# The last attention of an eight-layer model in half rounds: scores of one pair of kv heads at a time, a longer pipeline, and the second softmax's maximum taken inside the addition

## The chip, the cores and the metric

The kernel is one program on one core of a Trainium2 chip. It computes four blocks, each an attention and a feed-forward part, for eight sequences of 256 tokens of width 256, all in fp32 (masks and some one-hot matrices are bf16). The metric is the device time of one execution in microseconds. Engines are named as the profile names them: PE (TensorE matmul), PEld (its weight loads), DVE (VectorE), ACT (ScalarE), POOL (GpSimd) and SP (SyncE, which issues most DMAs).

## The reference

Only the last attention (L3) matters here. It is a differential attention: 16 query heads and 4 kv heads, each head with two parts of 16 columns. Each part has its own causal softmax; the second, weighted by a learned factor for each head, is subtracted from the first, and the difference, causal again, goes through one more softmax before it multiplies V.

```python
x = _layernorm(x + _L2_ffn_ref(x, ...), axis=-1)
x = _layernorm(x + _L3_attn_ref(x, Wq, Wk, Wv, Wo, lq1, lq2, lk1, lk2, rms_w), axis=-1)
x = _layernorm(x + _L3_ffn_ref(x, gate, gate_up_proj, down_proj), axis=-1)

def _L3_attn_ref(x, ...):              # 16 heads, 4 kv heads, D = 16
    q = _rope((x @ Wq).reshape(b, s, H, 2 * D))
    k = _rope((x @ Wk).reshape(b, s, KVH, 2 * D))
    v = (x @ Wv).reshape(b, s, KVH, D)
    ...                                # k and v repeated 4 times, heads cut in two parts
    energy = jnp.einsum('bqhad,bkhad->bahqk', qd, kd)
    energy = jnp.where(causal, NEG, energy)
    scores = jax.nn.softmax(energy / np.sqrt(D), axis=-1)
    diff = scores[:, 0] - lam * scores[:, 1]
    diff = jnp.where(causal, NEG, diff)
    diff = jax.nn.softmax(diff, axis=-1)
    att = jnp.einsum('bhqv,bvhd->bqhd', diff, v)
    att = att * jax.lax.rsqrt(jnp.mean(att * att, -1, keepdims=True) + EPS) * rms_w
    att = att * (1.0 - LAM_INIT)
    return att.reshape(b, s, E) @ Wo
```

## The kernel before

The eight layers run one after the other. The layers changed here are written in a manual schedule: on each engine the instructions stand in the order in which the Python code issues them, and the framework adds the waits. So the order of calls in the loop of `attn3` is the order of each engine's queue.

**Units.** `attn3` works on 48 units, six for each of the eight sequences (a batch, below). A unit is one block of 128 queries (`qc` 0 or 1) and some of the four heads that share a kv head: two heads with 128 keys when `qc` is 0 (two units), one head with 256 keys when `qc` is 1 (four units). All four kv heads, `s` in the code, are in each unit. The projections put kv head `s` in the 32 partitions from 32 s on, so the four score matmuls of a round use four 32-row strips of the PE array, and each writes its own PSUM bank.

**PSUM.** One pool has four tags of two banks each: `t` (projections, transposes), `a` and `s` (scores), `o` (two banks that `attn3` holds throughout: `bank_o` for the values, `bank_x` for V and the ends).

**What a unit does, by method of `Unit`:**
- `scores`: L651 matmuls for all four kv heads (two records each in the profile, since fp32 takes two passes), L664 a bf16 matmul that adds the causal mask, L668 a DVE reduction of each bank to the maximum, L671 the exponentials on ACT with their sums (each followed by an accumulator read).
- `factors`: L681 the reciprocals of the sums on DVE; on POOL L686, which masks the diagonal block, and L691 and L692, which make the factor `c` from the sums and the head's weight.
- `differences`, in two halves of two kv heads: L705 on DVE adds `c` times the second part's exponentials to the first's; L709 on DVE reduces the result to its maximum; L710 on POOL scales the maximum; L713 on POOL writes `v`, the scaled difference less its maximum.
- `turned`: L730 transposes `v` on PE, L732 takes the exponential on ACT straight from PSUM into `p`.
- `values`: L746 multiplies by V into `bank_o`, on 32-column strips; the ones beside V give the sum. L751 copies the result out when a query block is complete.

**The ends of a batch.** `finish(b)` is a generator whose steps the loop spreads over later units. It turns the result back (L764), divides (L768, L769), squares (L776), then does the RMS norm (L781 to L798), transposes (L805), multiplies by Wo (L814), adds the residual and normalizes. After the fourth batch it appends the sort of the next layer's tokens (`ffn3_sort`) to the queue `others`; that is router matmuls (L1959), top-4, ranks (`place`, L903 to L959) and then 32 row scatters issued by POOL (L986), three a unit.

**The loop.** In step n: `factors` of unit n-1, one step of `others`, `scores` of unit n, `values` of unit n-3, a projection step of the next batch (`project`: L607 matmuls, L611 DVE multiplication by the rotary tables, L625 V), `differences` of unit n-1 with another projection step and one step of `ends` between its halves, two steps of `others` unless rows are being scattered, `turned` of unit n-2. When the loop ends, what is left of `ends` and `others` is handed to `ffn3`, whose first fetch of rows (SP, L2012) waits for the scatter and for the last values.

## Time and profile before

| what | value |
|---|---|
| time, median of 3 runs | 2415.38 us (2408.47 to 2417.45) |
| the profiled execution | 2415.87 us, of it 2414.2 us span |
| busy in the span | PE 90%, DVE 59%, ACT 43%, POOL 38% |
| last attention, first L651 to last L746 | 1671.7 to 2102.8 us |
| an even batch in it (1813.4 to 1861.2 us) | 47.8 us; DVE 43.7, PE 42.5, ACT 34.8, POOL 33.2 busy |
| the batch with the sort beside it (1912.4 to 1978.6 us) | 66.2 us; DVE 57.2, PE 50.0 busy |
| granted PE clock in these two | 0.93 and 0.79 |

Busy shares over the whole span mix eight layers with different limits, so they say little of this one; a stretch of one batch is the right size, because all its work repeats every six units. PE's busy time counts a matmul from its start to a modelled end, so matmuls that overlap are counted once and short gaps vanish in it. For what PE's work really needs, one looks at how long after one group the next one starts when nothing is waited for. In the groups of instructions the columns are: line, engine, operation, output and input, shape, count; then busy us and mean ns of one; then the engine's idle time just before it, with what ended that. In the order of time they are start, duration, engine, line, operation.

### The profile page before, as it was taken

The page shows a single profiled execution, that of the slowest core. Times are in us where ns is not written, and L with a number is a line of the kernel's source. Part 1 is how long each engine was busy: PE and PEld are TensorE (multiplying, and loading weights), DVE is VectorE, ACT ScalarE, POOL GpSimd, SP SyncE. Part 2 cuts the span into 40 slices and gives each one's busy share as a digit, 9 for nine tenths or more (in the row PEclk, how much of TensorE's full clock was granted, in tenths as well). Part 3 has the DMA queues.
Part 4 walks back from the last instruction along what each step waited for, and adds up shares of the span by engine and source line. Part 5 has one row for each costly group of instructions (what it writes and reads, how often), then busy time and mean ns, then how long its engine had stood idle before and what let it go on. Part 6 is the DMA issues. An engine that isn't in the chain of part 4 may idle for free.

```text
span 2414.2 us, 36482 instructions
## 1 busy us (share of the span) xinstructions
PE 2166.5 (90%) x11920; PEld 1479.6 (61%) x11920; DVE 1432.6 (59%) x3998; ACT 1034.1 (43%) x2999; POOL 913.6 (38%) x1711
## 2 busy tenths in 40 slices
PE   7999889999999999999999999999889877689880
PEld 4555688857676676676654465556556654367760
DVE  4566486754644554544574444766998987553454
ACT  1334355554544544544441112223767746444340
POOL 1222444353433423433312311001666658616444
PEclk9999999999999999999999999999999978799995
DMA  5000411100000010000340011002000001255652
GB/s 166 1 1 1 168 41 46 46 24 3 3 3 3 3 54 1 1 1 1 131 160 1 0 53 54 1 1 107 1 2 1 2 3 43 67 149 189 214 174 81
DMA packets 92311, 120.78 MB, mean 50 GB/s; under 512 B 9757, under 2 KB 79582, under 8 KB 91102
## 3 DMA queue, kind: packets, MB, share of 16 engines
q1 hardware_dynamic: 82270, 95.75, 12.2%
q0 software_dynamic: 8192, 21.11, 2.8%
q8 instruction: 100, 1.64, 0.3%
q10 hardware_dynamic: 1664, 1.57, 0.2%
q14 instruction: 85, 0.70, 0.1%
HBM read 67.53 MB, written 50.88 MB: 49 GB/s over the span
## 4 chain that ended last, share of the span: by engine, by line
PE 26%; DVE 10%; POOL 7%; issue 3%; ACT 2%; DMA 2%; SPq 0%; POOLq 0%; another core or an unknown queue 0%; DVEq 0%; ACTq 0%
PE ps_a L2031 4%; PE ps_s L1842 2%; PE ps_a L1842 2%; POOL v L713 2%; PE ps_o L2053 2%; PE ps_a L1638 2%; PE ps_s L1638 2%; PE ps_o L1889 2%; DVE e L705 2%; ACT e L671 2%; DVE nmd L709 1%; DVE nm L668 1%; PE ps_t L2023 1%; POOL rows L986 1%; DVE bnst L200 1%
## 5 line engine op out<-in xcount | busy, mean ns | idle before, releaser
L1429 POOL TENSOR_SCALAR p<-p,rs 128x128 f32<-128x128 f32 (+1 forms) x256 | 104.9, 428 | 254.5 <-DVE rs L1427 155.8
L1419 ACT ACTIVATE p<-p,nms,rq 128x128 f32<-128x128 f32 (+1 forms) x256 | 137.7, 539 | 132.6 <-DVE nms L1415 132.3
L1343 ACT ACTIVATE sq<-ps_a 128x512 f32<-128x512 f32 x126 | 74.6, 592 | 195.5 <-PE ps_a L1335 195.2
L148 POOL TENSOR_SCALAR rsq<-bnmv 128x2 f32<-128x2 f32 x61 | 12.9, 211 | 379.3 <-DVE bnmv L201 364.1
L671 ACT ACTIVATE e<-ps_a,nm 128x128 f32<-128x128 f32 (+1 forms) x256 | 106.0, 437 | 105.6 <-DVE nm L668 95.6
L1344 DVE TENSOR_REDUCE ssk<-sq 128x4 f32<-128x512 f32 x64 | 43.8, 686 | 171.1 <-ACT sq L1343 170.9
L713 POOL TENSOR_SCALAR v<-e,r,nmd 128x128 f32<-128x128 f32 (+1 forms) x256 | 134.4, 537 | 10.0
L2031 PE MATMUL ps_a<-w_f_gup,xTg 128*128 x504 | 111.1, 344 | 17.0 <-DVE xTg L2025 5.9
L705 DVE SCALAR_TENSOR_TENSOR e<-e,c 128x128 f32<-128x128 f32 (+1 forms) x256 | 101.3, 446 | 38.9 <-POOL c L692 38.8
L1335 PE MATMUL ps_a<-w_a_wq,xT 128*128 128x512 f32 x256 | 122.5, 601 | 1.7 <-DVE k L1357 1.7
L1335 PE MATMUL ps_a<-w_a_wv,xT 128*128 128x512 f32 x256 | 120.8, 593 | 0.6 <-ACT q L1368 0.6
L1335 PE MATMUL ps_a<-w_a_wk,xT 128*128 128x512 f32 x248 | 116.5, 593 | 0.0
L1467 PE MATMUL ps_o<-w_a_wo,attT 128*128 128x256 f32 x512 | 111.8, 379 | 0.0
L730 PE MATMUL ps_t<-ident,v 128*128 128x128 f32 x384 | 68.7, 311 | 48.0 <-DVE qT L611 8.9
L671 ACT ACTIVATE e<-ps_s,nm 128x128 f32<-128x128 f32 (+1 forms) x256 | 107.1, 454 | 0.0
L1467 PEld LDWEIGHTS ps_o<-w_a_wo,attT 128*128 128x128 f32 x512 | 96.7, 190 | 12.8
L1195 DVE SCALAR_TENSOR_TENSOR yg<-ps_t,xg,yg 128x128 f32<-128x128 f32 x266 | 93.2, 350 | 17.9 <-PE ps_t L1184 8.4
L2031 PEld LDWEIGHTS ps_a<-w_f_gup,xTg 128*128 128x128 f32 x504 | 81.4, 195 | 29.6 <-issue 9.8
L1402 PE MATMUL ps_s<-kT,qT 128*128 128x256 f32 (+1 forms) x512 | 99.4, 327 | 0.0
L1344 DVE TENSOR_REDUCE ssq<-sq 128x4 f32<-128x512 f32 x64 | 43.8, 685 | 91.9 <-ACT sq L1343 91.9
L1184 PE MATMUL ps_t<-w_f_w,hg 128*128 x608 | 83.4, 281 | 10.1 <-DVE yg L1195 6.2
L730 PEld LDWEIGHTS ps_t<-ident,v 128*128 128x128 f32 x384 | 49.8, 160 | 64.5 <-POOL v L713 19.1
(418 smaller groups left out, 6008.7 us busy)
## 6 DMA issues: line engine op xcount, KB each, us to landing
rows<-zero SPq DMA_DIRECT2D x42, 384.0 KB
xg<-rows SPq DMA_DIRECT2D x42, 384.0 KB
outs<-yg SPq DMA_DIRECT2D x42, 384.0 KB
w_f_gup<-in_f_gup SPq DMA_DIRECT2D x8, 768.0 KB
w_f_w<-in_f_w SPq DMA_DIRECT2D x8, 512.0 KB
w_f_down<-in_f_down SPq DMA_DIRECT2D x8, 384.0 KB
w_f_up<-in_f_up SPq DMA_DIRECT2D x5, 512.0 KB
lrows<-zero SPq DMA_DIRECT2D x12, 204.0 KB
```

Of the source, the lines that this page charges most:

```text
L671: nc.scalar.activation(e[:, s, j * nk : (j + 1) * nk], sc[s][:, j, :], AF.Exp, bias=nm[:, s, j : j + 1], scale=1.0, accum_out=sums[:, s, j ...
L705: nc.vector.scalar_tensor_tensor(d[:, s, h, :], u.e[:, s, h, 1, :], u.c[:, s, h : h + 1], d[:, s, h, :], ALU.mult, ALU.add,)
L713: nc.gpsimd.tensor_scalar(u.v[:, s, h, :], d[:, s, h, :], u.r[:, s, h, 0:1], nm[:, s, h : h + 1], ALU.mult, ALU.add,)
L730: nc.tensor.transpose(ps[:, s, c, :], x, self.ident)
L1335: nc.tensor.matmul(ps, self.xt(u.b, t, c), w[which][:, c, u.cols], start=(c == 0), stop=(c == 1),)
L1402: nc.tensor.matmul(sc[:, j, :], u.qT[:, h0 + j, qc * P : (qc + 1) * P], u.kT[:, h0 + j, 0:nk], start=True, stop=True,)
L1419: nc.scalar.activation(u.p[qc][:, h0 + j, :], u.p[qc][:, h0 + j, :], AF.Exp, bias=nm[:, j : j + 1], scale=r[:, j : j + 1], accum_out=u.sum ...
L1429: nc.gpsimd.tensor_scalar(u.p[qc][:, j, :], u.p[qc][:, j, :], ri[:, j : j + 1], 1.0, ALU.mult, ALU.mult,)
L1467: nc.tensor.matmul(y[:, t, :], attTs[b][:, h, t * P : (t + 1) * P], w["wo"][:, h, :], start=(h == 0), stop=(h == 15),)
L1638: nc.tensor.matmul(x, xT[:, c, tok], w[name][:, c, cols], start=(c == 0), stop=(c == 1),)
L1842: nc.tensor.matmul(x, w[name][:, c, cols], xT[:, c, :], start=(c == 0), stop=(c == 1))
L2031: nc.tensor.matmul(ps, xT[j][:, c, :], w["gup"][:, bass.ds(er[j], 1), c, :].rearrange("p o f -> p (o f)"), start=(c == 0), stop=(c == 1),)
```

## The change

The score banks move into a pool of their own (`psum_as`), which is closed and opened again around `attn3`; inside it the pool holds two tiles of two banks, tag `pair`, instead of `a` and `s`. The tile of exponentials gets four buffers instead of three, and `v` is gone.

A unit is now done in two halves, each of one pair of kv heads:
- `scores(u, i)` does the matmuls of two strips into one pair of banks, both masks, one reduction over both banks and the exponentials.
- `factors` also multiplies, on POOL, the second part's exponentials by `c`, in place.
- `differences(u, i)` is one DVE operation for each head: it adds the two parts, scales by the first part's reciprocal and keeps the running maximum. POOL then casts the maxima to bf16.
- `turned(u, i)` transposes the differences and, into the same accumulation, multiplies the broadcast bf16 maximum by a negated identity (`nidentb`), which subtracts it from each column; then the exponential as before. The softmax does not depend on the value that is subtracted, so the rounded maximum serves.

In step n the loop does, for each half: `scores` of unit n, `turned` of unit n-3 (behind the matmuls, ahead of the reduction), in the second half `factors` of unit n-1, then `differences` of unit n-2 and projection, sort and end steps; `values` are those of unit n-4. The loop is one step longer. The first steps of `finish` become `gather`, called for each query block by itself, both through `bank_x`.

```diff
+    def open_pairs(self):
+        self.psum_as = self.pairs.enter_context(
+            self.tc.tile_pool(
+                name="psum_as", bufs=2, space=bass.MemoryType.PSUM, reuse_waits="tile"
+            )
+        )
+
     def ps(self, tag):
-        return self.psum.tile([P, 512], F32, tag=tag, name=f"ps_{tag}")
+        pool = self.psum_as if tag in "as" else self.psum
+        return pool.tile([P, 512], F32, tag=tag, name=f"ps_{tag}")
...
         bank_o, bank_x = self.ps("o"), self.ps("o")
+        nidentb = act.tile([P, P], BF16, tag="nidentb", name="nidentb", bufs=1)
+        nc.gpsimd.tensor_scalar(nidentb, self.identb, -1.0, None, ALU.mult)
...
-            def scores(u):
+            def scores(u, i):
 
                 qT, kT = qTs[u.b], kTs[u.b]
                 nk, nj = u.nk, 2 * u.nh
-                ps = [self.ps("as"[s % 2]) for s in range(4)]
+                if i == 0:
+                    u.nm = self.small.tile([P, 4, nj], F32, tag="nm3", name="nm3")
+                    u.sums = self.small.tile([P, 4, u.nh, 2], F32, tag="sums", name="sums")
+                    e = act.tile([P, 4, 512], F32, tag="e", name="e", bufs=4)
+                    u.e = e.rearrange("p s (h a k) -> p s h a k", h=u.nh, a=2)
+                two = slice(2 * i, 2 * i + 2)
+                ps = self.psum_as.tile([P, 2, 512], F32, tag="pair", name="ps_pair")
+                sc = ps.rearrange("p s (j k) -> p s j k", j=nj)
+                e = u.e[:, two].rearrange("p s h a k -> p s (h a) k")
+                sums = u.sums[:, two].rearrange("p s h a -> p s (h a)")
                 for j in range(nj):
-                    for s in range(4):
-                        r = slice(32 * s, 32 * s + 32)
+                    for s in range(2):
+                        r = slice(64 * i + 32 * s, 64 * i + 32 * s + 32)
                         nc.tensor.matmul(
-                            ps[s][:, j * nk : (j + 1) * nk],
+                            sc[:, s, j, :],
                             qT[r, 2 * u.h0 + j, u.qc * P : u.qc * P + P],
                             kT[r, j % 2, :nk],
                             start=(j == 0), stop=False,
                         )
-                nm = self.small.tile([P, 4, nj], F32, tag="nm3", name="nm3")
-                u.sums = self.small.tile([P, 4, u.nh, 2], F32, tag="sums", name="sums")
-                sums = u.sums.rearrange("p s h a -> p s (h a)")
-                e = act.tile([P, 4, 512], F32, tag="e", name="e", bufs=3)
-                u.e = e.rearrange("p s (h a k) -> p s h a k", h=u.nh, a=2)
-                sc = [x.rearrange("p (j k) -> p j k", j=nj) for x in ps]
-                for s in range(4):
+                for s in range(2):
                     nc.tensor.matmul(
-                        sc[s][:, :, nk - P :], self.identb, self.maskA[:, :nj, :],
+                        sc[:, s, :, nk - P :], self.identb, self.maskA[:, :nj, :],
                         start=False, stop=True,
                     )
-                    nc.vector.tensor_reduce(nm[:, s, :], sc[s], AX.X, ALU.max, negate=True)
-                for s in range(4):
+                yield
+                nm = u.nm[:, two]
+                nc.vector.tensor_reduce(nm, sc, AX.X, ALU.max, negate=True)
+                for s in range(2):
                     for j in range(nj):
                         nc.scalar.activation(
-                            e[:, s, j * nk : (j + 1) * nk], sc[s][:, j, :], AF.Exp,
+                            e[:, s, j, :], sc[:, s, j, :], AF.Exp,
                             bias=nm[:, s, j : j + 1], scale=1.0,
                             accum_out=sums[:, s, j : j + 1],
                         )
+                yield
 
             def factors(u):
 
                 g = nc.gpsimd
                 u.r = self.small.tile([P, 4, u.nh, 2], F32, tag="r3", name="r3")
                 nc.vector.reciprocal(u.r, u.sums)
-                u.c = self.small.tile([P, 4, u.nh], F32, tag="c3", name="c3")
-
+                c = self.small.tile([P, 4, u.nh], F32, tag="c3", name="c3")
+                g.tensor_tensor(c, u.sums[:, :, :, 0], u.r[:, :, :, 1], ALU.mult)
+                g.tensor_tensor(c, c, nlam[:, :, u.h0 : u.h0 + u.nh], ALU.mult)
                 for i in range(2):
                     diag = u.e[:, 2 * i : 2 * i + 2, :, 0, u.nk - P :]
                     g.affine_select(
                         diag, diag, pattern=[[0, 2], [0, u.nh], [-1, P]],
                         compare_op=ALU.is_ge, fill=NEG, base=0, channel_multiplier=1,
                     )
-                    if i == 0:
-                        g.tensor_tensor(u.c, u.sums[:, :, :, 0], u.r[:, :, :, 1], ALU.mult)
-                        g.tensor_tensor(
-                            u.c, u.c, nlam[:, :, u.h0 : u.h0 + u.nh], ALU.mult
-                        )
-
-            def differences(u):
-
-                d = u.e[:, :, :, 0, :]
-                u.v = act.tile([P, 4, u.nh, u.nk], F32, tag="v", name="v", bufs=3)
-                nm = self.small.tile([P, 4, u.nh], F32, tag="nmd", name="nmd")
-                for i in range(2):
-                    two = slice(2 * i, 2 * i + 2)
                     for s in (2 * i, 2 * i + 1):
                         for h in range(u.nh):
-                            nc.vector.scalar_tensor_tensor(
-                                d[:, s, h, :], u.e[:, s, h, 1, :], u.c[:, s, h : h + 1],
-                                d[:, s, h, :], ALU.mult, ALU.add,
-                            )
-                    nc.vector.tensor_reduce(nm[:, two], d[:, two], AX.X, ALU.max, negate=True)
-                    nc.gpsimd.tensor_tensor(nm[:, two], nm[:, two], u.r[:, two, :, 0], ALU.mult)
...
+                            x = u.e[:, s, h, 1, :]
+                            g.tensor_scalar(x, x, c[:, s, h : h + 1], 1.0, ALU.mult, ALU.mult)
+
+            def differences(u, i):
+
+                if i == 0:
+                    u.mx = self.small.tile([P, 4, u.nh], F32, tag="nmd", name="nmd")
+                    u.mb = [
+                        act.tile([P, 2, u.nh], BF16, tag="nmb", name="nmb", bufs=4)
+                        for _ in range(2)
+                    ]
+                for s in (2 * i, 2 * i + 1):
+                    for h in range(u.nh):
+                        d = u.e[:, s, h, 0, :]
+                        nc.vector.tensor_tensor_reduce(
+                            out=d, in0=d, in1=u.e[:, s, h, 1, :],
+                            scale=u.r[:, s, h, 0:1], scalar=2 * NEG,
+                            op0=ALU.add, op1=ALU.max, accum_out=u.mx[:, s, h : h + 1],
+                        )
+                nc.gpsimd.tensor_copy(u.mb[i], u.mx[:, 2 * i : 2 * i + 2])
+
+            def turned(u, i):
+
+                if i == 0:
+                    u.p = []
+                ps = self.ps("t").rearrange("p (s c q) -> p s c q", s=2, c=2)
+                for s in range(2):
+                    for c in range(2):
+                        x = (
+                            u.e[:, 2 * i + s, c, 0, :] if u.qc == 0
+                            else u.e[:, 2 * i + s, 0, 0, c * P : (c + 1) * P]
+                        )
+                        nc.tensor.matmul(
+                            ps[:, s, c, :], x, self.ident, is_transpose=True,
+                            start=(s == 0 and c == 0), stop=False,
+                        )
+                for s in range(2):
+                    for h in range(u.nh):
+                        most = u.mb[i][:, s, h : h + 1].to_broadcast([P, P])
+                        out, one = ps[:, s, h, :], nidentb
+                        if u.qc == 1:
+                            out = ps[:, s]
+                            one = nidentb.unsqueeze(1).to_broadcast([P, 2, P])
+                        nc.tensor.matmul(
+                            out, most, one, start=False, stop=(s == 1 and h == u.nh - 1)
+                        )
+                p = act.tile([P, 2, 2, P], F32, tag="p", name="p", bufs=4)
+                nc.scalar.activation(
+                    p.rearrange("p s c q -> p (s c q)"),
+                    ps.rearrange("p s c q -> p (s c q)"), AF.Exp,
+                )
+                u.p += [p[:, 0], p[:, 1]]
...
-                    if u.qc == 1:
-                        done.append(finish(u.b))
...
+        def gather(b, qc):
...
+            pt = bank_x.rearrange("p (h s d) -> p h s d", h=4, s=4)
...
         def finish(b):
...
+            if b == NB - 1:
+                gather(b, 1)
+                yield
+            att, sqs = atts[b], squares[b]
...
-        for n in range(len(units) + 3):
+        for n in range(len(units) + 4):
 
             def at(back):
                 return units[n - back] if 0 <= n - back < len(units) else None
 
-            u, last = at(0), at(1)
+            u = at(0)
             if u and u.qc == 0 and u.h0 == 0:
                 step(projections, 100)
                 if u.b + 1 < NB:
                     projections.append(project(u.b + 1))
-            if last:
-                last.factors()
-            step(others)
-            if u:
-                u.scores()
-            step(self.late)
-            if at(3):
-                at(3).values()
-            step(projections)
-            halves = last.differences() if last else iter(())
-            next(halves, None)
-            if u and u.qc == 0:
-                step(projections)
-            step(ends)
-            next(halves, None)
-            next(halves, None)
-            if not self.scattering:
-                step(others, 2)
-            if at(2):
-                at(2).turned()
-            ends += done
-            done.clear()
+            for i in range(2):
+                soft = u.scores(i) if u else iter(())
+                next(soft, None)
+                if at(3):
+                    at(3).turned(i)
+                next(soft, None)
+                if i == 1 and at(1):
+                    at(1).factors()
+                if at(2):
+                    at(2).differences(i)
+                if i == 0:
+                    step(projections)
+                    step(self.late)
+                    step(others)
+                    continue
+                if at(4):
+                    at(4).values()
+                if u and u.qc == 0:
+                    step(projections)
+                step(ends)
+                b, back = divmod(n - 8, len(units) // NB)
+                if b >= 0 and back == 0:
+                    gather(b, 0)
+                if b >= 0 and back == 2:
+                    gather(b, 1)
+                    ends.append(finish(b))
+                if not self.scattering:
+                    step(others, 2)
+        ends.append(finish(NB - 1))
         return ends + others
...
                 elif name == "attn3":
+                    m.pairs.close()
+                    m.open_pairs()
...
                     left = m.attn3(w, act, kept[i], start=start, beside=beside)
+                    m.pairs.close()
+                    m.open_pairs()
```

## The prediction

> **What bounds the kernel now.** I read the page's busy shares first, then busy time by stretch, the groups by shape in three equal batches, the TensorE order in time, and the waits. The changed stage is the last attention, from 1671.7 us (first L651) to 2102.8 us (last L746): eight batches of six units.
>
> ```profile
> PE 2166.5 (90%) x11920; PEld 1479.6 (61%) x11920; DVE 1432.6 (59%) x3998; ACT 1034.1 (43%) x2999; POOL 913.6 (38%) x1711
> PEclk9999999999999999999999999999999978799995
> ```
>
> Over the whole span PE leads; the dip of the granted clock at the right is the second half of this attention. The stage itself, by stretch (us, then busy time of PE, PEld, DVE, ACT, POOL, then clock, DMA share, GB/s):
>
> ```profile
> 1813.40:1861.20 47.80, 42.50 (x362) 29.80 (x360) 43.72 (x94) 34.80 (x147) 33.22 (x82) 0.93 0.00 1
> 1861.20:1909.10 47.90, 42.46 (x362) 29.84 (x360) 44.47 (x96) 34.35 (x146) 33.20 (x82) 0.93 0.01 2
> 1912.40:1978.60 66.20, 50.04 (x382) 35.70 (x381) 57.15 (x156) 35.42 (x147) 38.62 (x91) 0.79 0.01 3
> 1978.60:2035.50 56.90, 44.76 (x384) 31.43 (x383) 43.64 (x95) 34.42 (x145) 43.38 (x87) 0.89 0.10 34
> 2035.50:2092.00 56.50, 37.79 (x277) 22.77 (x275) 39.66 (x87) 34.80 (x146) 48.85 (x101) 0.82 0.12 40
> ```
>
> Each line is about one batch. An even batch takes 47.8 us with DVE busy 44.2: DVE is the bound. The batch with the sort beside it takes 66.2, again DVE first (57.2); in the last two, which issue the scatter, POOL is nearly full, since each L986 row (1.0 us) has a gap of about 0.3 us that is not counted. By shape, in three even batches:
>
> ```profile
> L713 POOL TENSOR_SCALAR v<-e,r,nmd 128x256 f32<-128x256 f32 x48 | 27.9, 591 | 2.5
> L705 DVE SCALAR_TENSOR_TENSOR e<-e,c 128x256 f32<-128x256 f32 x49 | 24.4, 538 | 11.2 <-POOL c L692 11.2
> L730 PE MATMUL ps_t<-ident,v 128*128 128x128 f32 x145 | 24.1, 303 | 13.0 <-DVE qT L611 4.5 <-ACT p L732 4.3 <-POOL nmd L710 2.4
> L709 DVE TENSOR_REDUCE nmd<-e 128x2 f32<-128x512 f32 x24 | 16.5, 686 | 0.8
> L668 DVE TENSOR_REDUCE nm<-ps_s 128x2 f32<-128x512 f32 x24 | 16.3, 681 | 0.0
> ```
>
> L709 is what the change removes; L705 waits 3.7 us a batch for POOL. Now TensorE, one round of scores in order of time:
>
> ```profile
> 1839.82 0.48 PE L651 MATMUL ps_a<-kT,qT 32*128 32x256 f32 x1
> 1839.83 0.48 PE L651 MATMUL ps_s<-kT,qT 32*128 32x256 f32 x1
> 1839.83 0.48 PE L651 MATMUL ps_a<-kT,qT 32*128 32x256 f32 x1
> 1839.84 0.48 PE L651 MATMUL ps_s<-kT,qT 32*128 32x256 f32 x1
> 1840.14 0.37 PE L651 MATMUL ps_a<-kT,qT 32*128 32x256 f32 x1
> ...
> 1840.57 0.37 PE L651 MATMUL ps_a<-kT,qT 32*128 32x256 f32 x1
> ...
> 1840.90 0.28 PE L664 MATMUL ps_a<-maskA,identb 128*128 128x256 bf16 x1
> 1841.02 0.27 PE L664 MATMUL ps_s<-maskA,identb 128*128 128x256 bf16 x1
> ```
>
> Four 32-row strips start within 0.02 us of each other and step together every 0.215 us. A strip that comes late runs alone at its own pace, as the first attention shows:
>
> ```profile
> 53.77 0.59 PE L398 MATMUL ps_s<-qT,kT 32*128 32x512 f32 x1
> ...
> 53.83 0.69 PE L398 MATMUL ps_s<-qT,kT 32*128 32x512 f32 x1
> ...
> 54.36 0.59 PE L398 MATMUL ps_s<-qT,kT 32*128 32x512 f32 x1
> ```
>
> The pass at 54.36 took 0.59 us with no fp32 strip beside it, like the one at 53.77 that had company: a strip gains nothing from idle neighbours.
>
> **PE's work in an even batch, from start to next start.** A unit of the first query block: scores 1.12, mask 0.97, values 0.57, two projections 3.56, eight transposes 0.99, sum 7.2. Of the second: 1.08, 0.54, 0.57, 1.02, sum 3.2, and 1.83 for a projection in two of four. With V (0.94), L814 (1.73), L156 (0.5), L764 (0.95) and L805 (0.6): 2 x 7.2 + 4 x 3.2 + 2 x 1.83 + 4.7 = 35.6 us. The other 12.2 of 47.8 are waits and a slow clock (0.93 granted).
>
> **The change on PE.** Scores by half rounds: the strip keeps its passes, so a half with two strips costs what the round with four did. Bounds: nothing, if what paces PE is the count of instructions (that stays), and a whole round more, +1.12 or +1.08; the row at 54.36 decides for the second. [...] The mask is as many matmuls with one more hand-over (+0.09); transposes in two groups +0.1. New matmuls that subtract the maximum: eight of 128 columns a unit in the first block, four of 256 in the second. No row is of 128 columns in bf16; the weight load of L664 (106 ns) and its 256-column pitch (0.11) bound them from 0.06 to 0.11. I take 0.11: +0.9 and +0.45. So +2.2 and +1.8 a unit, 2 x 2.2 + 4 x 1.8 = +11.6 a batch, and PE needs **47.2 us where a batch takes 47.8**.
>
> **The change on DVE, ACT, POOL.** L709 goes: 12 x 0.60 (its pitch) = 7.2 a batch. 24 reductions of 512 become 12 of 1024: the nearest rows are 1.225 us (L1858, 128x1024) and twice 0.68; saves up to 1. L705 becomes an addition with a running maximum, as L1408 does it now:
>
> ```profile
> L1408 DVE CUSTOM_DVE_ANT_0 p<-ps_s,tri 128x256 f32<-128x256 f32 x128 | 49.1, 421 | 4.4 <-PE ps_s L1402 4.3
> L1408 DVE DVE_READ_ACCUMULATOR2_ANT nm<- 128x1 f32 x256 | 21.5, 84 | 0.0
> ```
>
> That reads PSUM, here both operands are in SBUF: between L1408's 0.42 + 0.08 and L705's 0.54 + 0.08, even. DVE falls from 44.2 to 34 to 38 a batch. ACT keeps its work (34.5). POOL swaps L713 for a product of the same shape (0.43 to 0.59 as L713 spreads) and L710 (0.22) for a cast (L903's 0.28): 33 a batch still. All three are then under PE, which hides them; without that cover DVE's saving is the gain.
>
> **New waits.** The addition waits for POOL's product, issued one unit earlier; behind it on DVE stand the projection's multiplication, which frees the ps_t bank that PE writes next, and the next reduction. Behind a 128-column unit POOL ends its first half (0.2 + 0.4 + 0.64 + 4 x 0.49 = 3.2 us after the reciprocal) just as DVE asks. PE's subtraction waits for the cast, a unit older. The pair of banks: 1.4 scores and mask, 0.3 hand-over, 1.2 reduction, 2.8 exponentials (8 x 0.355) = 5.7 us against a 9.4 us unit; 1.4 + 0.3 + 1.2 + 1.8 = 4.7 against 4.9 in the shortest. No step waits for one issued just before it, so I give PE 1.3 us of waits a batch, half of what L730 now waits for DVE and ACT (8.8 in three batches): **48.5**.
>
> **The sum**, against the profiled execution (2415.9 us, span 2414.2; 0.5 above the median of 2415.4):
> - Five batches before the sort took 46.2, 47.1, 47.8, 47.8 and 47.9 from first reduction to first reduction, 236.8 in all; 5 x 48.5 = 242.5: **+5.7**. Ends -0.8 (5 x 47.2) and +28 (half of the 12.2 stays: 53).
> - Sort batch: 48.5 + 5.4 of sort matmuls (L1959 3.6, L926 1.8) + 7 of the 11.2 that PE waits for r_ones (5.3) and before L975 (5.9) = 61, since DVE has 10 us less queued: **-5**. Ends -12 and +2.
> - Two scatter batches: 18 L986 rows of 1.3 us on 33 of POOL work make 56 by themselves: **-1**. Ends -5 and +3.
> - Drain: the last reduction ends at 2083.0, the last values at 2102.8. Afterwards the chain is exponentials 1.8, reciprocal to first products 2.4, second products 1.5, additions 1, cast, turn, exponential, values 3: about 10.5, but POOL arrives late with row 32, now one unit later, ahead of the last products: **-3**. Ends -9 and +1.
> - Nothing for the negated identity (one POOL operation at the start), the reopened PSUM pools (at the end 8.8 us of w_f_down and 9.5 us of xg cover them; up to +2 without), and the ends through one bank: the same instructions, spread over units, and the sort begins one unit later. SP keeps its order; its first fetch still waits for the last values.
>
> Sum -3.3: **2412 us**, no change that a measurement of this kernel tells (0.5% is 12 us).
>
> **Rivals.**
> *PE packs and the late batches gain* (faster). For: every wait crosses a unit. Against: no stretch of this attention has PE without gaps. 47.2 a batch (-0.8), sort without its long waits -10, scatter -3, drain -6: -20, 2395 us.
> *PE does not pack* (slower): half rounds give it twelve hand-overs a batch where six were, and half of the 12.2 us stays: 53 a batch, +28, sort -2: 2442 us. It decides from 51.6 a batch (5 x 51.6 - 236.8 - 9 = +12). For: a wait on PE has no slack left to hide in.
> *The clock stays low* (slower). Now each even batch has 6.8 us at half clock, 3.4 lost. If that stays, 51.9 a batch: +22.7, sort 0, late ones -3: 2435 us. Against: it goes with PE's gaps, which should close. [...]
> *The DVE saving does not come.* Each of the 32 additions a batch would have to cost 0.3 to 0.4 us more than its nearest rows (0.50 and 0.62) before DVE passes PE's 47.2. Nothing in the rows points there; no chance of its own.
>
> **Chances.** No change 0.45 (own range 2403 to 2427), PE packs 0.25, does not pack 0.2, clock 0.1. Faster 0.25, same 0.45, slower 0.3; the range takes in most of both sides, 2394 to 2440.
>
> **What would show it.** Right: even batches of 48 to 49 us, PE busy over 45 in them, DVE under 38, half rounds at the pitch of full ones, clock near 1.0. Wrong: L651's successor pacing faster with two strips, PE idle behind ACT's exponentials or POOL's cast, POOL no longer full in the scatter batches.

## The result and the profile after

The changed kernel takes 2386.07 us (median of 4 runs, 2381.64 to 2390.56) beside 2412.98 us for the kernel before: a ratio of 0.9889, 95% interval 0.986 to 0.9917. It is faster by 1.1%, where no change was forecast (2412 us, range 2394 to 2440). The profiled run took 2390.56 us (span 2388.6), against 2415.87 (span 2414.2) before.

The page's busy shares and granted clock (tenths, in 40 slices of the span):

```profile
PE 2198.7 (92%) x12176; PEld 1520.3 (64%) x12176; DVE 1376.3 (58%) x4062; ACT 1038.6 (43%) x2999; POOL 892.7 (37%) x1712
PEclk9999999999999999999999999999999988699995
```

TensorE has more to do (2198.7 us for 2166.5) in a shorter span, DVE less. The stage itself by stretch, from the changed kernel's trace (us; busy time of PE, PEld, DVE, ACT, POOL with counts; then granted clock, DMA share, GB/s). The first line is the first batch, the next two are even ones, then the batch with the sort and the first one with the scatter:

```profile
1675.10:1711.70 36.60, 33.76 (x269) 24.18 (x266) 32.13 (x87) 30.70 (x135) 22.21 (x57) 1.00 0.13 53
1753.60:1798.30 44.70, 44.63 (x394) 33.48 (x393) 36.51 (x103) 35.08 (x147) 30.75 (x81) 1.00 0.01 2
1798.30:1843.00 44.70, 44.63 (x394) 33.48 (x393) 35.88 (x102) 35.37 (x148) 30.73 (x81) 1.00 0.01 2
1887.70:1949.30 61.60, 61.60 (x469) 46.55 (x468) 47.17 (x150) 37.91 (x155) 34.57 (x92) 0.86 0.00 1
1949.30:1999.90 50.60, 43.71 (x362) 31.86 (x361) 40.60 (x116) 34.32 (x142) 38.09 (x81) 0.94 0.09 30
```

An even batch takes 44.7 us in place of 47.8, and TensorE is busy for 44.63 of them at full clock: it has no gap left, and is the bound. DVE fell from 44.2 to 36.2. The order of TensorE in one half round, from the timeline of its matmuls (start, duration, instruction):

```profile
1805.81 1.16 PE L673 MATMUL ps_pair<-kT,qT 32*128 32x128 f32 x16
1806.90 0.60 PE L680 MATMUL ps_pair<-maskA,identb 128*128 128x512 bf16 x2
1807.35 0.60 PE L744 MATMUL ps_t<-ident,e 128*128 128x128 f32 x4
1807.78 0.38 PE L755 MATMUL ps_t<-nidentb,nmb 128*128 128x256 bf16 x2
1808.00 0.38 PE L620 MATMUL ps_t<-xT,w_a_wq 128*128 128x256 f32 x1
```

From start to next start: half a round of scores with two strips 1.09 us (the whole one with four took 1.12), the mask 0.45, four transposes 0.43, the maximum 0.22. What waited for whom in three even batches (total us, times, longest):

```profile
POOL c L702 <- DVE r L700: 27.2, 15, 2.9
ACT p L759 <- PE ps_t L755: 19.7, 23, 2.8
DVE nm L686 <- PE ps_pair L680: 15.3, 22, 1.4
...
PEld ps_pair L673 <- ACT e L689: 1.7, 3, 0.6
```

By shape, in the same three batches (count, busy time, mean ns of one, idle time before with its releaser):

```profile
L689 ACT ACTIVATE e<-ps_pair,nm 128x256 f32<-128x256 f32 x97 | 44.8, 479 | 3.8 <-DVE nm L686 3.8
L686 DVE TENSOR_REDUCE nm<-ps_pair 128x4 f32<-128x1024 f32 x24 | 29.2, 1216 | 5.2 <-PE ps_pair L680 5.1
L726 DVE CUSTOM_DVE_ANT_0 e<-e,r 128x256 f32<-128x256 f32 x48 | 23.7, 530 | 0.0
L713 POOL TENSOR_SCALAR e<-e,c 128x256 f32<-128x256 f32 x49 | 23.3, 485 | 0.0
L755 PE MATMUL ps_t<-nidentb,nmb 128*128 128x128 bf16 x48 | 4.6, 219 | 0.0
```

The joined addition L726 costs what L705 did (530 ns for 538), the product L713 costs POOL less than the scaled difference L713 of before (485 for 591), and the 219 ns in the row of L755 overlap: four 128-column subtractions start within 0.22 us. The other engines wait for TensorE; TensorE's own waits are fractions of a microsecond. By stretches of the two profiled executions, from first reduction to first reduction:

| stretch (us) | before | after | difference | forecast |
|---|---|---|---|---|
| first batch | 46.2 | 36.5 | -9.7 | |
| second | 47.1 | 42.0 | -5.1 | |
| three even ones | 143.5 | 134.1 | -9.4 | |
| these five | 236.8 | 212.6 | -24.2 | +5.7 |
| with the sort | 66.2 | 61.6 | -4.6 | -5 |
| first with the scatter | 56.9 | 50.6 | -6.3 | -1 (both scatter batches) |
| last batch and drain, to the last values | 67.2 | 75.7 | +8.5 | -3 (drain) |
| the rest, after the attention | 311.4 | 312.9 | +1.5 | 0 |

### The profile page after: what moved, and what is told of

It is laid out like the page before. It is cut to its first block, busy times and chain, and to the rows that moved or that the text cites. A ratio compares the mean times of both kernels' runs of the same rounds, so it can differ in the third digit from the quotient of the medians.

```text
span 2388.6 us, 37056 instructions
## 1 busy us (share of the span) xinstructions
PE 2198.7 (92%) x12176; PEld 1520.3 (64%) x12176; DVE 1376.3 (58%) x4062; ACT 1038.6 (43%) x2999; POOL 892.7 (37%) x1712
## 5 line engine op out<-in xcount | busy, mean ns | idle before, releaser
L689 ACT ACTIVATE e<-ps_pair,nm 128x256 f32<-128x256 f32 (+1 forms) x512 | 208.2, 437 | 14.9 <-DVE nm L686 14.6
L686 DVE TENSOR_REDUCE nm<-ps_pair 128x4 f32<-128x1024 f32 (+1 forms) x96 | 117.0, 1219 | 47.5 <-PE ps_pair L680 46.4
L1382 DVE TENSOR_REDUCE ssk<-sq 128x4 f32<-128x512 f32 x64 | 43.8, 686 | 170.9 <-ACT sq L1381 170.8
L673 PE MATMUL ps_pair<-kT,qT 32*128 32x256 f32 (+1 forms) x1024 | 117.0, 359 | 2.0 <-ACT e L689 1.6
L726 DVE CUSTOM_DVE_ANT_0 e<-e,r 128x128 f32<-128x128 f32 (+1 forms) x256 | 108.7, 469 | 14.1 <-POOL e L713 14.1
L689 ACT ACTIVATION_READ_ACCUMULATOR e<-ps_pair,nm 128x1 f32 x512 | 114.3, 223 | 0.0
L713 POOL TENSOR_SCALAR e<-e,c 128x128 f32<-128x128 f32 (+1 forms) x256 | 108.9, 437 | 0.0
L673 PEld LDWEIGHTS ps_pair<-kT,qT 32*128 32x128 f32 x1024 | 79.6, 196 | 31.2 <-issue 19.7
L1382 DVE TENSOR_REDUCE ssq<-sq 128x4 f32<-128x512 f32 x64 | 43.8, 685 | 90.2 <-ACT sq L1381 89.5
```

The costliest lines, as they stand in the source:

```text
L673: nc.tensor.matmul(sc[:, s, j, :], qT[r, 2 * u.h0 + j, u.qc * P : u.qc * P + P], kT[r, j % 2, :nk], start=(j == 0), stop=False,)
L686: nc.vector.tensor_reduce(nm, sc, AX.X, ALU.max, negate=True)
L689: nc.scalar.activation(e[:, s, j, :], sc[:, s, j, :], AF.Exp, bias=nm[:, s, j : j + 1], scale=1.0, accum_out=sums[:, s, j : j + 1],)
L713: g.tensor_scalar(x, x, c[:, s, h : h + 1], 1.0, ALU.mult, ALU.mult)
L726: nc.vector.tensor_tensor_reduce(out=d, in0=d, in1=u.e[:, s, h, 1, :], scale=u.r[:, s, h, 0:1], scalar=2 * NEG, op0=ALU.add, op1=ALU.max, ...
```

## What was to be found out

Two things were missed: five batches came out 30 us better than forecast, the end 6 us worse. Theory A after the result: TensorE's instruction stream is now all that bounds an even batch, and the gain is that its waits went. Rival B, the prediction's reading: DVE was the bound, its relief is the gain, and half rounds are only a cost.

Each ratio below is to the kernel before, measured beside the run. The medians of before differ (2391.8 to 2417.1 us). This fits what stands behind this attention: it takes 285 to 292 us in the profiles of e1 to e4 and e13 to e15, 308 to 318 in the others. So stages are compared by their own stretches.

For each kernel the mean of three steady batches (the third to the fifth) is split in three: TensorE's **packed** work, summed from start to next start (35.6 us before, 44.6 after; for the others worked out from these: half rounds 6.4, maximum matmuls 3.2); the **clock** loss, half of the time in which half the clock was granted (an upper bound, as TensorE may wait in it); and the rest, **waits**. The three columns say where TensorE's time goes; whether a batch waits for it has to be read from the trace.

| kernel | ratio (95% interval) | batch | packed | clock | waits |
|---|---|---|---|---|---|
| before | 1 | 47.8 | 35.6 | 3.4 | 8.8 |
| changed | 0.9889 (0.986 to 0.9917) | 44.7 | 44.6 | 0 | 0.1 |
| e1 before, no maximum | 0.9858 (0.9838 to 0.9879) | 43.8 | 35.6 | 0 | 8.2 |
| e2 before, half rounds | 1.0228 (1.0202 to 1.0254) | 52.7 | 42.0 | 2.8 | 7.9 |
| e3 before, longer distance | 1.0057 (1.0037 to 1.0077) | 51.4 | 35.6 | 4.6 | 11.2 |
| e4 changed, full rounds | 1.0184 (1.0159 to 1.0208) | 53.2 | 38.2 | 5.0 | 10.0 |
| e5 changed, turns in a block | 1.0562 (1.054 to 1.0584) | 71.9 | 44.6 | 11.9 | 15.3 |
| e6 changed, shorter distance | 1.0164 (1.0147 to 1.0181) | 55.7 | 44.6 | 6.8 | 4.3 |
| e7 changed, no maximum | 0.981 (0.9794 to 0.9827) | 42.9 | 41.4 | 0 | 1.5 |
| e11 changed, old order | 1.0046 (1.0026 to 1.0067) | 54.2 | 44.6 | 6.3 | 3.3 |
| e12 changed, old additions | 1.0022 (0.9998 to 1.0046) | 47.1 | 41.4 | 2.3 | 3.4 |
| e13 e11 with one step moved | 0.9968 (0.9957 to 0.9979) | 46.9 | 44.6 | 0 | 2.3 |

## Experiments on the kernel before: one part of the change at a time

**e1, DVE's saving alone.**

```diff
-  nc.vector.tensor_reduce(nm[:, two], d[:, two], AX.X, ALU.max, negate=True)
-  nc.gpsimd.tensor_tensor(nm[:, two], nm[:, two], u.r[:, two, :, 0], ALU.mult)
...
-      nm[:, s, h : h + 1], ALU.mult, ALU.add,
+      1.0 / 256.0, ALU.mult, ALU.mult,
```

> The kernel before, with the maximum of the differences left out: L709's reductions and L710 go, L713 multiplies by r and by 1/256 in place of subtracting (so the output is another). DVE has 7.2 us a batch less, nothing else moves. If DVE was the bound of the even batches (my prediction's reading), they fall from 47.8 to 42 to 44 us and the kernel by 20 to 30 us. If DVE's 44.2 of 47.8 was a chain of waits through PE, ACT and POOL, they stay above 46.5 us and the kernel loses less than 10 us.

Measured: 2356.99 us against 2393.07, and even batches of 43.8. An even one by stretch:

```profile
1802.10:1846.10 44.00, 39.38 (x362) 28.25 (x361) 36.13 (x83) 34.90 (x146) 28.40 (x69) 1.00 0.00 1
```

The numbers are what B expected: 4.0 us a batch went, with 7.7 us less to do for DVE, which stands at 36 of 44. In the split 3.4 of the 4.0 are the slow clock (0.93 became 1.00) and 0.6 are waits, but the trace of the kernel before does not let the slow clock be charged. In its three steady batches DVE is busy for 44.2 us of each 47.8 and waits for TensorE for less than 0.3. Its one large wait in a batch, 2.8 us, is for POOL's factor, and it falls into the stretch at half clock (1806.8 to 1813.6 us in the first of the three). From the waits of two batches, then from the timeline:

```profile
DVE e L705 <- POOL c L692: 5.6, 2, 2.8
```

```profile
1805.74 0.74 DVE L781 TENSOR_REDUCE ms<-asq 128x16 f32<-128x256 f32 x2
...
1808.68 0.25 POOL L792 TENSOR_TENSOR ms<-ms,rr 128x32 f32<-128x32 f32 x1 [0.67 <-ACT rr L791]
...
1809.99 1.20 POOL L798 TENSOR_TENSOR att<-att,rr 128x256 f32<-128x256 f32 x2
...
1813.19 0.21 POOL L692 TENSOR_TENSOR c<-c,nlam 128x4 f32<-128x4 f32 x1
1813.44 1.00 DVE L705 SCALAR_TENSOR_TENSOR e<-e,c 128x256 f32<-128x256 f32 x2 [2.81 <-POOL c L692]
```

The factor stands in POOL's queue behind the RMS norm of the batch that ended, which goes from DVE through POOL and ACT and back, and POOL's waits in this stretch are for those two, not for TensorE. So B was right about the kernel before: DVE, with this one wait, held the batch, and TensorE's waits and half clock lay in time that it had to spare. With DVE's load gone the next chain stands 4.0 us behind; which one it is was not taken apart. The batch is even 0.9 us shorter than the changed kernel's 44.7, but this run computes no maximum at all.

**e2, half rounds alone**, with the changed kernel's pairs of banks and reductions of 1024:

```diff
-  ps = [self.ps("as"[s % 2]) for s in range(4)]
+  for i in range(2):
+      ps = self.psum_as.tile([P, 2, 512], F32, tag="pair", name="ps_pair")
...
-          for s in range(4):
-              r = slice(32 * s, 32 * s + 32)
+          for s in range(2):
+              r = slice(64 * i + 32 * s, 64 * i + 32 * s + 32)
...
-  nc.vector.tensor_reduce(nm[:, s, :], sc[s], AX.X, ALU.max, negate=True)
+      nc.vector.tensor_reduce(nm[:, two], sc, AX.X, ALU.max, negate=True)
```

> The kernel before, with the scores alone by half rounds through pairs of banks and reductions of 1024; additions, turns and ends as before. PE has 6.5 us a batch more work. By my prediction (half rounds are only a cost) the even batches stay at 47.8 to 51 us, DVE at 43 to 44 busy. If what PE waited for was the four banks held by the exponentials, they fall to 44 to 46.5 us although PE has more to do.

Measured: 52.7 us a batch, above both expectations. TensorE's work rose by 6.4 and the batch by 4.9: waits and slow clock fell only from 12.2 to 10.7. That waits for the four banks alone held the old kernel back is refuted; here half rounds are a cost, as B said.

**e3, the longer distance alone.**

```diff
-  for n in range(len(units) + 3):
+  for n in range(len(units) + 4):
...
-  if at(3):
-      at(3).values()
+  if at(4):
+      at(4).values()
...
-  if at(2):
-      at(2).turned()
+  if at(3):
+      at(3).turned()
```

> The kernel before, with turns three units back and values four, nothing else (one more v buffer, one p buffer less). If PE's waits for POOL's v and ACT's p (8.8 us in three batches) were the gap, the even batches fall by up to 3 us, to 45 to 47. If they only stood in for the bound elsewhere, 47.8 stays. The drain grows by 3 to 8 us, the first batch shrinks by as much.

Measured: 51.4 us in the steady batches (44.7 in the second alone), worse than either expectation; 9.1 us a batch at half clock against 6.8. More distance doesn't remove waits by itself. Why they grew here stays open; the run also has one buffer of `p` less, which was not tried apart.

So of the three parts none but DVE's relief gains alone, and two lose.

## Experiments on the changed kernel: one part taken back

**e4, full rounds.** Four strips at once into both pairs of banks, all else by halves:

```diff
+  if i == 0:
+      u.sc = [self.psum_as.tile([P, 2, 512], F32, tag="pair", ...) for _ in range(2)]
       for j in range(nj):
-          for s in range(2):
-              r = slice(64 * i + 32 * s, 64 * i + 32 * s + 32)
+          for s in range(4):
+              r = slice(32 * s, 32 * s + 32)
```

> The changed kernel with full rounds: all four strips of a unit's scores at once into both pairs of banks, maxima, exponentials, additions and turns by halves as they are. PE needs 6 x 1.08 = 6.5 us a batch less, 38.2 in place of 44.7. If half rounds are only a cost, the even batches fall to 39 to 42 us and the kernel by 15 to 35 us. If it is the second set of banks that lets PE run without gaps, PE waits again for the exponentials and the even batches are 44 to 48 us, PE 38 busy.

Measured: 53.2 us, above both expectations and 8.5 more than with half rounds, although TensorE has 6.4 us less to do. The waits in two batches show why (total, times, longest):

```profile
PEld ps_pair L676 <- ACT e L696: 20.8, 12, 2.1
PE ps_pair L676 <- ACT e L696: 16.6, 12, 1.8
```

The weight loads and the matmuls wait side by side, once a unit, for the exponentials that still read the banks. The second pair of banks is what lets the scores run ahead: half rounds are worth their 6.4 us here and weren't in e2, so B was wrong that they are only a cost.

**e5, the turns in one block behind the scores.**

```diff
   for i in range(2):
       soft = u.scores(i) if u else iter(())
       next(soft, None)
-      if at(3):
-          at(3).turned(i)
       next(soft, None)
+  if at(3):
+      at(3).turned(0)
+      at(3).turned(1)
```

with the additions of both halves after it, then projections, values and ends.

> The changed kernel with the same half rounds, reductions, additions and distances between units, but not woven: both halves of the scores, then both halves of the turns, then the additions, as the kernel before had its order. If weaving the turns and projections between the half rounds is what leaves PE without gaps (my theory now), PE waits again for the ps_t banks and for the exponentials ahead of them in ACT's queue, and the even batches go from 44.7 to 47 to 53 us. If half rounds, joined additions and the longer distance are enough by themselves, 44.7 stays.

Measured: 71.9 us, far above the 47 to 53 that were expected. The expectation calls this the order of the kernel before, which it isn't: there the turns stand at a unit's end. As built, both ps_t banks are filled right behind the scores, and the projection waits for their exponentials, which ACT reaches only after both halves of the scores':

```profile
PEld ps_t L620 <- ACT p L759: 35.0, 8, 5.9
PE ps_t L620 <- ACT p L759: 33.0, 8, 5.6
```

That is 5.9 us at worst, eight times in two batches. The fair test of the order is e11.

**e6, the shorter distance**, turns two units back, values three:

```diff
-  if at(3):
-      at(3).turned(i)
+  if at(2):
+      at(2).differences(i)
   next(soft, None)
...
-  if at(4):
-      at(4).values()
+  if at(3):
+      at(3).values()
```

and the turns of at(2) after the projections in each half.

> The changed kernel with the turns two units back and the values three, put behind the additions in each half round (the additions ahead of the reduction on DVE). If the distance is needed, PE waits for additions and cast and the even batches are 46.5 to 52 us; the drain is 4 to 8 us shorter and the first batch as much longer. If the distance is not needed, 44.7 stays.

Measured: 55.7 us, above the 46.5 to 52 that were expected if the distance is needed. The waits are only 4.3 of that; 6.8 are the clock (13.6 us of each batch at half). The drain is shorter as expected (last batch and drain 69.4 against 75.7), the first batch longer (46.3 against 36.5).

**e7, no maximum.**

```diff
-  nc.gpsimd.tensor_copy(u.mb[i], u.mx[:, 2 * i : 2 * i + 2])
...
-  nc.tensor.matmul(
-      out, most, one, start=False, stop=(s == 1 and h == u.nh - 1)
-  )
...
-      ps.rearrange("p s c q -> p (s c q)"), AF.Exp,
+      ps.rearrange("p s c q -> p (s c q)"), AF.Exp, scale=1.0 / 256.0,
```

> The changed kernel without the matmuls that subtract the maximum and without their cast (the exponent is scaled by 1/256 in their place, so the output is another). PE has 6 x 0.53 = 3.2 us a batch less, POOL 3.0, DVE the same. If PE alone bounds the even batches now, they fall by just that, 44.7 to 41.4 to 42 us. If a chain through ACT or DVE stands close behind it, they stay above 43.5.

Measured: 42.9 us, between the two expectations: of the 3.2 us taken from TensorE 1.8 come out, 1.4 turn into waits. TensorE is the bound, so theory A is right about what holds the changed kernel, but a chain through the other engines stands close behind it. The late batches gained more (first with the scatter 45.3, last and drain 69.5), though no scatter row was touched; that led to e9.

**e12, the old additions in the new order.** Multiply and add, reduction and POOL's subtraction as before, no maximum matmuls:

```diff
-  nc.vector.tensor_tensor_reduce(
-      out=d, in0=d, in1=u.e[:, s, h, 1, :], ...
+  nc.vector.scalar_tensor_tensor(
+      d[:, s, h, :], u.e[:, s, h, 1, :], u.c[:, s, h : h + 1],
+      d[:, s, h, :], ALU.mult, ALU.add,
+  )
+  nc.vector.tensor_reduce(nm[:, two], d[:, two], AX.X, ALU.max, negate=True)
```

> The changed kernel's weaving, half rounds and distances with the old additions: multiply and add on DVE, a reduction for the maximum, the subtraction on POOL, no matmuls for it. PE needs 44.7 - 3.2 = 41.5 us a batch, DVE 36.2 + 7.2 = 43.4. If the joined addition was needed, the even batches are 47 to 53 us. If the order alone makes the gain, they are 43.5 to 45.5 us with DVE nearly without gaps, and the new maximum is worth nothing in them.

Measured: 47.1 us with DVE busy 43.4 of it, and no change against the kernel before as a whole. The joined addition is needed: it costs TensorE 3.2 us a batch and is still worth 2.4.

## The order, one gap, and the clock

**e11, the changed kernel's instructions in the old order.**

```diff
+  if at(1):
+      at(1).factors()
+  step(others)
   for i in range(2):
       soft = u.scores(i) if u else iter(())
       next(soft, None)
-      if at(3):
-          at(3).turned(i)
       next(soft, None)
...
       if at(2):
+          at(2).differences(1)
...
+      if at(3):
+          at(3).turned(0)
+          at(3).turned(1)
```

> The changed kernel's instructions in the order that the kernel before had: factors first, both halves of the scores, values, projections, first additions, second additions, and the eight turns of a unit at its end. Half rounds, joined additions and distances stay. If the weaving is what lets PE run without gaps, the even batches are 48 to 58 us. If half rounds, joined additions and distance do it by themselves, 44.7 to 46.

Measured: 53.2, 54.7 and 54.7 us, 10 more than woven. TensorE's timeline shows a single gap of more than half a microsecond, at the unit that transposes X (idle time before an instruction and its releaser in brackets):

```profile
1843.43 0.60 PE L167 MATMUL ps_t<-ident,X 128*128 128x128 f32 x4
1844.38 0.66 PE L744 MATMUL ps_t<-ident,e 128*128 128x128 f32 x4 [0.35 <-DVE qT L624]
1844.88 0.39 PE L755 MATMUL ps_t<-nidentb,nmb 128*128 128x128 bf16 x4
1847.42 1.11 PE L744 MATMUL ps_t<-ident,e 128*128 128x128 f32 x4 [2.16 <-ACT xT L133]
1848.33 0.63 PE L755 MATMUL ps_t<-nidentb,nmb 128*128 128x128 bf16 x4
1848.89 2.08 PE L673 MATMUL ps_pair<-kT,qT 32*128 32x256 f32 x8
```

The second four turns need the bank of L167, which ACT frees with the copy L133, behind eight exponentials. The gap is 2.16 us. From 1847.4 to 1861.0 the trace then grants half the clock: a half round takes 2.01 us to the next start where it takes 1.06 at full clock in the same trace. That is 13.7 us at half speed, up to 6.8 lost, three times the gap.

The clock fell behind gaps of 0.35 and 2.16 us, and it stayed low for 13.7 us although TensorE was busy for 13.32 of the 13.70 us from 1848.3 to 1862.0 (granted clock 0.53 there, 1.00 in the 3.4 us after).

**e13, one step moved**, against e11:

```diff
-      step(ends)
...
       if at(3):
           at(3).turned(0)
           at(3).turned(1)
+      step(ends)
```

> The kernel of the old order with one line moved: the step of the ends (with the transposes of X, L167, whose bank ACT frees behind eight exponentials) comes after the eight turns in place of before them. If the single gap of 2.2 us and the 13.7 us at half clock that follow it are the whole loss, both go and the even batches fall from 54.7 to 44.7 to 47 us at a clock of 1.0. If blocks of half rounds and of turns cost by themselves, they stay above 50.

Measured: 46.9 us in each of the three batches, in e11 and here by stretch:

```profile
1813.10:1867.80 54.70, 51.69 (x394) 37.51 (x396) 36.03 (x104) 35.31 (x147) 29.72 (x80) 0.88 0.00 1
```

```profile
1807.10:1854.00 46.90, 46.04 (x394) 33.32 (x396) 37.08 (x103) 35.05 (x147) 30.11 (x81) 1.00 0.01 2
```

The first line is e11, the second e13. The same instructions in almost the same order; the clock went from 0.88 to 1.00 and 7.8 us are gone. So the old order isn't slow by its blocks: the one gap and its slow clock made most of the loss, and weaving is worth the last 2.2 us. (Its batch with the sort is longer, 70.1 us, so that the whole kernel gains only 0.3% on before.)

## The late batches

**e8, the products on DVE beside the scatter.**

```diff
-  g.tensor_scalar(x, x, c[:, s, h : h + 1], 1.0, ALU.mult, ALU.mult)
+  by = nc.vector if self.scattering else g
+  by.tensor_scalar(x, x, c[:, s, h : h + 1], 1.0, ALU.mult, ALU.mult)
```

> The changed kernel with the product L713 on DVE in place of POOL for the units that stand beside the scatter (about 32 a batch, 0.42 us each on POOL). If POOL bounds these two batches and the drain, the time from the first reduction after the sort to the last values falls from 126 to 105 to 118 us, the kernel by 8 to 21 us, and the even batches are untouched. If PE or the waits across the engines bound them, it stays within 3 us.

Measured: ratio 0.9953 (0.9936 to 0.9969). The late time (from the first reduction after the sort to the last values) rose from 126.3 to 142.9 us, outside both expectations. The product (L714 there) stands in DVE's queue ahead of the additions, and it needs POOL's factors of the same unit. The timeline of POOL and DVE at one of them:

```profile
1972.40 0.24 DVE L700 RECIPROCAL r<-sums 128x16 f32<-128x16 f32 x1
1972.98 0.96 POOL L1025 DMA_INDIRECT rows<-X,r_slots  x1 [0.30 <-issue]
1974.26 0.96 POOL L1025 DMA_INDIRECT rows<-X,r_slots  x1 [0.31 <-issue]
1975.24 0.21 POOL L702 TENSOR_TENSOR c<-sums,r 128x8 f32<-128x8 f32 x1
1975.53 0.20 POOL L703 TENSOR_TENSOR c<-c,nlam 128x8 f32<-128x8 f32 x1
...
1975.77 2.41 DVE L714 TENSOR_SCALAR e<-e,c 128x128 f32<-128x128 f32 x8 [3.12 <-issue]
```

The factors stand behind scatter rows; DVE idles 3.12 us for them with the additions of another unit behind. The trace gives no releaser here ("issue"), but the product starts 0.04 us after L703 ends. So do eight others, and the nine idle times add up to 32.8 us in the late batches.

Work moved to a free engine together with its wait for the busy one made that engine wait too.

**e9, only the cast of the maxima on DVE.**

```diff
-  nc.gpsimd.tensor_copy(u.mb[i], u.mx[:, 2 * i : 2 * i + 2])
+  nc.vector.tensor_copy(u.mb[i], u.mx[:, 2 * i : 2 * i + 2])
```

> The changed kernel with the cast of the maxima (L731) on DVE behind the additions, in place of POOL; output as before. If the late batches lose by PE's waits for this cast behind POOL's scatter rows (40 us of waits for it between the sort and the end), the time from the first reduction after the sort to the last values falls from 126 to 112 to 120 us and the kernel by 6 to 14 us; the even batches, bound by PE, stay at 44.7. If POOL's rows and products bound the late batches by themselves, it stays within 3 us.

Measured: ratio 0.9876 (0.9853 to 0.9898); the late time fell to 117.0 us as expected, the even batches rose to 45.1. In the time of the whole kernel the gain is not clear of noise (the changed kernel had 0.9889, 0.986 to 0.9917).

**e10, cast and products on DVE** (the products only beside the scatter), each product directly ahead of its addition, a unit after its factors:

```diff
+  if u.c is not None:
+      x = u.e[:, s, h, 1, :]
+      nc.vector.tensor_scalar(
+          x, x, u.c[:, s, h : h + 1], 1.0, ALU.mult, ALU.mult
+      )
```

> The kernel of the cast on DVE, with the products of the units beside the scatter on DVE too, directly ahead of each addition, so that DVE no longer waits for POOL's factors in the same unit. If POOL bounds the late batches, they fall by 5 to 12 us more; if PE or the chain of a unit does, nothing more is gained, and if DVE's 0.3 to 0.4 us a product lies on the chain, some of the gain of the cast goes back.

Measured: ratio 0.9872 (0.9848 to 0.9896), late time 117.9. Nothing more is gained: with some 14 us a batch of products off POOL (32 of 0.38 to 0.50 us) the two scatter batches are no shorter, so POOL's busy time isn't the bound there. Which chain is was not taken apart.

**e14, the cast on DVE only beside the scatter**, and **e15, the changed kernel again**, on one chip:

```diff
-  nc.gpsimd.tensor_copy(u.mb[i], u.mx[:, 2 * i : 2 * i + 2])
+  by = nc.vector if self.scattering else nc.gpsimd
+  by.tensor_copy(u.mb[i], u.mx[:, 2 * i : 2 * i + 2])
```

> The changed kernel with the cast of the maxima on DVE only for the units beside the scatter. If the cast behind POOL's rows is what the late batches lose by, the even batches keep 44.7 and the late time falls from 126 to 115 to 119 us: 8 to 11 us under the changed kernel in the same call. If e9's gain needed the cast on DVE from the start, less.

> The changed kernel itself, beside the one with the late cast on the same chip: 0.986 to 0.992 of the kernel before, as it was measured.

Measured: e14 2359.12 us, 0.9855 (0.9839 to 0.9872); e15 2366.07 us, 0.9884 (0.9867 to 0.9901). The even batches are 44.7 in both, the late time 120.0 against 126.1; the largest waits of TensorE for POOL in e15, from the sort's end to the end:

```profile
PEld L755 <- POOL nmb L731: 17.3, 8, 6.0
PE ps_t L755 <- POOL nmb L731: 14.9, 6, 5.8
```

In e14 one of 2.6 us is left; TensorE's largest waits for POOL are then for the ends (att, 11.9 us). The gain is 7.0 us between the medians, a little under the 8 to 11 that were expected, with ranges that don't touch (2357.44 to 2359.95 and 2362.87 to 2367.09): a kernel that computes the same and is faster than both.

## Why the prediction was wrong, step by step

- **What bounds the kernel now.** "DVE is the bound" of an even batch holds: DVE was busy or waiting for POOL's factor for 47.0 of 47.8 us. (That wait is 2.8 us a batch, not 3.7: the 11.2 us in the row of L705 hold four waits, as one stands at each edge of the three batches.) The wrong steps are behind it, in what the new kernel needs.
- **The change on PE.** "PE needs 47.2 us" was 2.6 too much. This is the step that failed first. The doubling of the scores was right (1.06 to 1.09 us a half round; the row at 54.36 was the right one to decide by). Mis-sized were the hand-overs: turns in two groups take 0.88 us a unit where I took 1.09 and 1.12, masks 0.88 and 0.46 where I took 1.06 and 0.63. The rows that I added 0.1 to were longer already than two of the new groups. The maximum matmuls took 0.53 a unit in both blocks, against 0.9 and 0.45: a 128-column one took 0.056 us from start to start where a 256-column one took 0.109 (four in 0.22 us), the lower of my bounds and not the upper. The sum has a slip as well: the terms of the second block add up to 1.7, not 1.8 (0.3 us a batch).
- **New waits.** 1.3 us a batch for TensorE (half of the 8.8 in three batches would be 1.5); there is 0.1. In TensorE's account the change bought 9.0 us of packed work with 12.1 of waits and clock, where I had 11.6 against 10.9: a sign turned by two small terms on either side.
- **The change on DVE, ACT, POOL.** Right: DVE 36.2 (34 to 38 was given), ACT 35. POOL came down to 30.7, where 33 was forecast, since L713 took 0.38 and 0.48.
- **The sum, five batches.** -24.2 against +5.7. Of the 30, 19 are five times the 3.8 us a batch above. The other 11 are a term that was left out: the sum charged all five at the full price, and the first two take 36.5 and 42.0 us, 10.9 below the steady 44.7 (before: 2.3). That they have less to issue, with turns and values a unit further back, fits the counts (269 and 378 matmuls in their stretches where a steady batch has 394) but is argued: in e6, at the short distance, the first two are 13.8 below its steady ones as well.
- **Sort batch.** -4.6 against -5, right in size, not in its parts: TensorE is busy for all of 61.6 us at a clock of 0.86, so that the 7 us of waits that were left in the sum are a slow clock of up to 8.6.
- **Scatter and drain.** +2.2 together against -4. That the drain holds what the first batches didn't do is argued in the same way. And TensorE waited up to 6.0 us at a time for the cast, a new operation on POOL. The step on new waits had said that "PE's subtraction waits for the cast, a unit older", and not what stands ahead of it in POOL's queue: at the longest wait three scatter rows (3.6 us from the first start) and then a unit's factors, masks and products (3.4). e14 shows its price: 6.1 us of late time.
- **The rivals.** *PE packs and the late batches gain* (0.25) had the even batches right in kind, and that its total of -20 lies near the measured -25.3 is luck: its five batches were -0.8 where -24.2 came, its sort -10 where -4.6 came, its scatter and drain -9 where +2.2 came. *The clock stays low* was worth its place, as e11 shows what one gap does to a kernel that TensorE bounds; in the even batches the clock is 1.00 and no gap is left. That it goes with TensorE's gaps holds in e13 (one gap of 2.16 us less, 0.88 to 1.00), but half the clock was no loss in the kernel before, and in its steady batches (6.8 us at 0.50) the clock stayed low for a second 3.41 us after 0.3 us idle in the first. *PE does not pack* gave 53 a batch; e11 has 54.2, though by one gap a batch and the clock behind it, not by twelve hand-overs.

## What to carry to other kernels

Ask first which engine's queue never waits for the others: it was DVE in the even batches before and is TensorE now. The waits and the slow clock of another engine are not lost time by themselves (12.2 us of TensorE's a batch in the kernel before, with DVE busy for 44.2 of 47.8). Once TensorE is the bound, price a gap on it by what the clock does after it: in e11 2.2 us idle cost up to 6.8 more. Two parts that each lose alone can then be needed together (half rounds and the longer distance here). Sum an engine's new work from rows without waits in them, and look at both ends of a deeper pipeline, where the first batches came out shorter (-9.7 and -5.1 us here) and the last longer (+8.5). An operation put on a busy engine's queue has to be priced behind what stands ahead of it there (TensorE waited up to 6.0 us for the cast), not by its own 0.2 us.

## What was not expected of the hardware

In the traces of the two kernels the granted clock changed in steps of 3.41 us: every stretch at one clock lasted a whole number of them, the last of each trace aside. Between 1670 and 2070 us, these windows of 3.41 us were sorted by how long no matmul ran in them. Of 167 windows at full clock that were followed by another, nine in ten had 0.82 us idle or less and none more than 1.70. Of the 21 that the clock fell after, half had 1.83 or more and none all of its 3.41. Nor does the idle time of one window tell it alone: the falls in the three steady batches of the kernel before come after 0.59 us idle, in gaps of at most 0.22. All 20 windows after which it came back had at most 0.32 us idle, and nine in ten at most 0.04. As matmul ends are modelled, single windows are uncertain.
